# Layer 1's attention: the transposes of the probabilities and the values' product one row of scores later, the rotation of the queries behind the second row

## The chip, the cores and the metric

One core of a Trainium2 chip runs the whole program: four small transformer layers with different attention and feed-forward parts, as a single launch. The metric is the device time of that launch in microseconds. Its engines work in parallel, each through its own instruction stream in order: TensorE (PE, matmuls and transposes; its weight loads are shown apart as PEld), VectorE (DVE), ScalarE (ACT), GpSimd (POOL) and SyncE (SP), the last two here mostly issuing transfers. An instruction waits on semaphores for what it needs from other engines, and everything behind it on its engine waits with it.

## The reference

The input is x of 4 sequences, 512 tokens, 256 channels, in float32. Each of the four layers computes `x = x + attention(layernorm(x)) + ffn(layernorm(x))`. The change is in layer 1's attention, a latent attention with 16 heads:

```python
q = _rmsnorm(x @ wq_a, q_a_ln_w) @ wq_b            # 192 latent -> 16 heads x (128 + 64)
q_nope, q_pe = (q[..., :D_NOPE], q[..., D_NOPE:])
ckv = x @ wkv_a
compressed_kv, k_pe = (ckv[..., :KV_LORA], ckv[..., KV_LORA:])   # 64 + 64
kv = _rmsnorm(compressed_kv, kv_a_ln_w) @ wkv_b
k_nope, v = (kv[..., :D_NOPE], kv[..., D_NOPE:])
q_pe, k_pe = rope(q_pe), rope(k_pe)                 # rotation: x * cos + half_swapped(x) * sin
scores = jnp.einsum('bqhd,bkhd->bhqk', qf, kf) * softmax_scale   # causal
attn = jax.nn.softmax(scores, axis=-1)
out = jnp.einsum('bhqk,bkhd->bqhd', attn, v)
return out.reshape(b, s, N_HEADS * D_V) @ wo
```

Layer 1's feed-forward part is a mixture of 512 tiny experts chosen by product keys (8 per token, whose rows are gathered from memory), plus a dense gated unit. Layer 2's routing starts while layer 1 still runs.

## The kernel before, in words

The residual x and its normalised transpose xnT stay on chip. Layer 1 is written as four Python generators, which `weave` (L566) interleaves: each `yield` names a cost, and the stream with the smallest share of its declared total goes next. They are latent attention (`latent_pieces`, L1071, total 457), product keys and experts (`product_key_pieces`, 237), the dense unit (`glu_units`, 126) and layer 2's first routing (`room`, 270, from 0.915 of its total on). The order in which the generators write instructions is the priority that a list scheduler works with: it puts each engine's stream into its final order by readiness in a model of its own, so an instruction may stand earlier or later on its engine than it was written. Instructions marked with `keep_in_program_order` keep their order among each other.

Latent attention is computed with the key up-projection folded into the queries, and the value up-projection into the output weights. A *head* s here is one of 16 heads of one of 4 sequences: 64 of them, in 32 pairs; even and odd s make a pair. kf holds keys (64 latent channels and 64 rotated ones) of all tokens, cv the 64 latent value channels.

- `queries(p)` makes the queries of pair p: two PE products of two matmuls each (L1129 to L1134), a copy of the rotary part on ACT (L1137, pes), four transfers on SP that swap its halves of 32 (psw<-pes, L1139), and two scaled copies on ACT into qf (L1141, L1142).
- `rotate` finishes them on DVE: pes times cosine (L1148), psw times sine (L1149), two sums into qf (L1150, L1151).
- `probabilities(s, i)` makes row block i (128 queries) of head s against its (i + 1) x 128 keys: the score matmul on PE (L1042), mask and minimum on DVE (L1045), exponential and sum on ACT (L1049). After row 2 the reciprocals of the first three sums are taken on DVE (L1165) and the three tiles scaled on ACT (L1167), after row 3 the fourth. A *row of scores* is one such row block; a head has four. The tiles are called pr0 to pr3, with two buffers each.
- `turned(s, j)` transposes, on PE (L1174), key block j of the probabilities, out of the tiles j to 3, into one PSUM bank of two (tag tr), and returns a copy into PT (L1178): on DVE for even j (512 and 256 wide), on ACT for odd j (384 and 128). The copy of one j is written behind the transposes of the next.
- The values' product (L1328) multiplies the PT tiles of both heads of a pair with cv, eight matmuls; both heads run side by side in the two halves of PE's columns. ACT scales the result into zT (L1334).
- `out_pieces` multiplies the zT of two pairs with the output weights (L1282) and adds to x on DVE (L212).

The main loop runs over s from 0 to 64 and, inside, over the rows i. A step (s, i) writes row i of head s's scores, then `turned(s - 1, i)`, then the copy that was left from the step before, and yields 0.85. At odd s and i = 0 the rotation of the next pair's queries comes before that yield; at even s and i = 0 `queries` follows it, with a yield of 2.6. Every second step also lets a piece of `out_pieces` run. After the four steps of an even s (from 2 on) comes the values' product of heads s - 2 and s - 1, with a yield of 2.1:

```python
if s > 0:
    ...
    ready, copy = copy, turned(s - 1, i)
    if ready:
        ready()
if i == 0 and s % 2 == 1 and s < 63:
    rotate(*turning)
yield 0.85
```

Line numbers are those of the kernel before, unless said otherwise.

Of the kernel before, what the change touches and what calls it, by code (L numbers as in the profile page):

```python
# [16 lines left out]
P = 128  # L17
NB, SEQ, DM = 4, 512, 256
NT = NB * SEQ
NTILE = NT // P  # L20
TPB = SEQ // P
# [1049 lines left out]
def latent_pieces(c, a, keep, open_pool):  # L1071
# [20 lines left out]
    pool = open_pool()  # L1092
    weights = {}

    def carry(g):

        w = c.unit(a["l_units"][g])
        wqT, wkT, wvT = v3(w[:, :768], QL), v3(w[:, 768:1024], KL), v3(w[:, 1024:1280], KL)
        wo = v3(w[:, 1792:2816], DM)
        pw, pv = c.ps(), c.ps()  # L1100
        for h in range(4):
            hk = slice(h * KL, (h + 1) * KL)
            nc.tensor.matmul(pw[:, hk], lhsT=wqT[:, h, :P], rhs=wkT[:, h, :], start=True, stop=True)
            nc.tensor.matmul(
                pv[(h % 2) * KL : (h % 2 + 1) * KL, (h // 2) * DM : (h // 2 + 1) * DM],
                lhsT=wvT[:, h, :], rhs=wo[:, h, :], start=True, stop=True,
            )
        pw1 = c.ps()
        for h in range(4):
            hk = slice(h * KL, (h + 1) * KL)  # L1110
            nc.tensor.matmul(pw1[KL:, hk], lhsT=wqT[:, h, P:], rhs=wkT[:, h, :], start=True, stop=True)
        wl0 = c.tile(pool, [P, 256], "wl0")
        wl1 = c.tile(pool, [P, 256], "wl1")
        wz = c.tile(pool, [P, 2, DM], "wz")
        nc.scalar.copy(wl0, pw[:, :256])
        nc.scalar.copy(wl1[KL:, :], pw1[KL:, :256])
        nc.scalar.copy(wz, v3(pv, DM))
        weights[g] = w[:, 1280:1536], w[:KL, 1536:1792], wl0, wl1, wz

    def queries(p):  # L1120

        g, b, pair = p // 8, p // 2 % 4, p % 2
        if p % 8 == 0:
            carry(g)
        wpe0, wpe1, wl0, wl1, _ = weights[g]
        tokens = slice(b * SEQ, (b + 1) * SEQ)
        cols = slice(pair * P, (pair + 1) * P)
        pe, pl = c.ps(), c.ps()
        nc.tensor.matmul(pl, lhsT=wl0[:, cols], rhs=qa0[:, tokens], start=True, stop=False)  # L1129
        upper = nc.tensor.matmul(pe, lhsT=wpe1[:, cols], rhs=qa1[:KL, tokens], start=True, stop=False)  # L1130
        with tc.issue_after(upper.ins), tc.high_priority(offset=200):
            nc.tensor.matmul(pl, lhsT=wl1[KL:, cols], rhs=qa1[KL:, tokens], start=False, stop=True)
        with tc.high_priority(offset=100):
            nc.tensor.matmul(pe, lhsT=wpe0[:, cols], rhs=qa0[:, tokens], start=False, stop=True)  # L1134

        pes, psw = (c.tile(pool, [P, SEQ], n, bufs=1) for n in ("pes", "psw"))
        nc.scalar.copy(pes, pe)  # L1137
        for to in range(0, P, 32):
            nc.sync.dma_start(psw[to : to + 32, :], pes[to ^ 32 : (to ^ 32) + 32, :])  # L1139
        qf = c.tile(pool, [P, 2, SEQ], "qf")  # L1140
        nc.scalar.mul(qf[:KL, 0, :], pl[:KL, :], -scale)  # L1141
        nc.scalar.mul(qf[KL:, 1, :], pl[KL:, :], -scale)  # L1142
        qfs[p] = qf
        return pes, psw, qf

    def rotate(pes, psw, qf):
        pec = c.tile(pool, [P, SEQ], "pec", bufs=1)
        nc.vector.tensor_mul(pec, pes, cosq)  # L1148
        tc.keep_in_program_order(nc.vector.tensor_mul(psw, psw, sinq))  # L1149
        nc.vector.tensor_add(qf[:KL, 1, :], pec[:KL, :], psw[:KL, :])  # L1150
        nc.vector.tensor_add(qf[KL:, 0, :], pec[KL:, :], psw[KL:, :])  # L1151

    def probabilities(s, i):
        p, h = s // 2, s % 2
        b = p // 2 % 4
        if i == 0:
            totals[s] = c.tile(pool, [P, TPB], "total")
        rinv = totals[s]
        prs[s].append(exp_scores(
            c, pool, late, qfs[p][:, h, :], kf[:, h, b * SEQ : (b + 1) * SEQ], i, rinv[:, i : i + 1]  # L1160
        ))
        if i >= TPB - 2:

            done = slice(0, i + 1) if i < TPB - 1 else slice(i, i + 1)
            nc.vector.reciprocal(rinv[:, done], rinv[:, done])  # L1165
            for j in range(TPB)[done]:
                nc.scalar.mul(prs[s][j], prs[s][j], rinv[:, j : j + 1])  # L1167

    def turned(s, j):

        pt = c.ps("tr")
        n = SEQ - j * P
        for i in range(j, TPB):
            nc.tensor.transpose(  # L1174
                pt[:, (i - j) * P : (i - j + 1) * P], prs[s][i][:, j * P : (j + 1) * P], c.ident
            )
        copy = nc.scalar.copy if j % 2 else nc.vector.tensor_copy
        return lambda: copy(PTs[s][:, START[j] : START[j] + n], pt[:, :n])  # L1178

    START = (0, 512, 896, 1152)  # L1180
    qfs, prs, totals, PTs, zTs = {}, {}, {}, {}, {}
# [84 lines left out]
    turning = queries(0)  # L1266
# [23 lines left out]

    copy, pieces = None, iter(())
    yield 1.9
    for s in range(65):
        if s < 64:
            prs[s] = []
        for i in range(TPB):
            if s < 64:
                probabilities(s, i)
            if s > 0:
                if i == 0:  # L1300
                    PTs[s - 1] = c.tile(pool, [P, 1280], "PT")
                ready, copy = copy, turned(s - 1, i)
                if ready:
                    ready()
            if i == 0 and s % 2 == 1 and s < 63:
                rotate(*turning)
            yield 0.85
            if i % 2:
                yield from islice(pieces, 1)
            if i == 0 and s % 2 == 0 and s < 62:  # L1310
                turning = queries(s // 2 + 1)
                yield 2.6
        if copy:
            copy()
            copy = None
        if s > 0:
            del prs[s - 1]
        if s % 2 == 1:
            continue
        if s == 0:  # L1320
            continue

        p = s // 2 - 1
        g, b, pair = p // 8, p // 2 % 4, p % 2
        z = c.ps("acc")
        for j in range(TPB):
            for h in range(2):
                tc.keep_in_program_order(nc.tensor.matmul(  # L1328
                    z[h * KL : (h + 1) * KL, j * P :], lhsT=cv[:, b * TPB + j, :],
                    rhs=PTs[s - 2 + h][:, START[j] : START[j] + SEQ - j * P],  # L1330
                    start=(j == 0), stop=(j == TPB - 1),
                ))
        zTs[pair] = c.tile(pool, [P, SEQ], "zT", bufs=3)
        nc.scalar.mul(zTs[pair], z, kv_w)  # L1334
        yield 2.1
        if pair == 1:
            pieces = out_pieces(g, b)
# [1176 lines left out]
```

## Time and profile before

| | |
|---|---|
| median of 3 runs | 2913.95 us (2909.5 to 2915.22) |
| profiled execution | 2915.69 us |
| its span, first to last instruction | 2913.9 us |
| mean granted TensorE clock | 0.996 |
| busy share of the span: PE, DVE, ACT, POOL | 98%, 73%, 48%, 30% |
| layer 1's attention stage, 845 to 1450 us: PE, DVE, ACT busy | 588.7, 494.6, 411.8 of 605 us |

The profile is one execution, recorded instruction by instruction. Its page gives busy times, the chain of work that ended last and the costliest groups; the trace behind it also answers with tables by stretch of time, with lists of who waited for whom, and with the instructions in order of time. In the list of waits a line reads "engine, tile and line that waited, the engine, tile and line that released it: total us, number of times, longest". In the order of time a line has the start and length in us, engine, line, operation, out<-in, shapes and count, and in brackets the idle time before it with what ended it. PE's matmuls are pipelined and the ends shown are modelled, so a PE that shows as busy is not always at its peak.

### The profile page before, as it was taken

The page shows a single profiled execution, that of the slowest core. Times are in us where ns is not written, and L with a number is a line of the kernel's source. Part 1 is how long each engine was busy: PE and PEld are TensorE (multiplying, and loading weights), DVE is VectorE, ACT ScalarE, POOL GpSimd, SP SyncE. Part 2 cuts the span into 40 slices and gives each one's busy share as a digit, 9 for nine tenths or more (in the row PEclk, how much of TensorE's full clock was granted, in tenths as well). Part 3 has the DMA queues.
Part 4 walks back from the last instruction along what each step waited for, and adds up shares of the span by engine and source line. Part 5 has one row for each costly group of instructions (what it writes and reads, how often), then busy time and mean ns, then how long its engine had stood idle before and what let it go on. Part 6 is the DMA issues. An engine that isn't in the chain of part 4 may idle for free.

```text
span 2913.9 us, 40511 instructions
## 1 busy us (share of the span) xinstructions
PE 2860.2 (98%) x13767; PEld 1920.8 (66%) x13767; DVE 2131.7 (73%) x5421; ACT 1401.9 (48%) x3354; POOL 862.4 (30%) x687
## 2 busy tenths in 40 slices
PE   9999999999999999999999999999999999999999
PEld 5566665666655655555577688888888756666666
DVE  6778778787778787888775687777777666666666
ACT  4444445454366666667733554444444333333332
POOL 0565655656510033333035100000000043333331
PEclk9999999999999999999999999999999999999999
DMA  2433333333320144444234544444444300000000
GB/s 106 119 109 115 113 98 95 109 116 97 109 82 17 54 101 124 116 107 112 79 120 120 164 118 125 144 130 130 147 124 141 102 1 22 22 22 22 22 1 30
DMA packets 138687, 268.60 MB, mean 92 GB/s; under 512 B 19729, under 2 KB 99105, under 8 KB 134129
## 3 DMA queue, kind: packets, MB, share of 16 engines
q1 hardware_dynamic: 124016, 218.20, 24.4%
q0 software_dynamic: 14176, 47.04, 6.5%
q8 instruction: 109, 1.79, 0.3%
q14 instruction: 98, 0.79, 0.1%
q10 hardware_dynamic: 288, 0.79, 0.1%
HBM read 202.25 MB, written 54.26 MB: 88 GB/s over the span
## 4 chain that ended last, share of the span: by engine, by line
PE 59%; DVE 7%; ACT 4%; DMA 2%; issue 1%; SPq 0%; POOL 0%; DVEq 0%; ACTq 0%
PE mm L358 17%; PE acc L358 7%; PE mm L1042 6%; PE tr L358 6%; PE acc L1709 5%; PE acc L1058 4%; PE mm L177 3%; PE acc L266 1%; PE acc L1328 1%; DVE pr L1045 1%; PE tr L1174 1%; ACT pr L1049 1%; PE mm L185 1%; PE mm L2121 1%; ACT pr L1167 1%
## 5 line engine op out<-in xcount | busy, mean ns | idle before, releaser
L1049 ACT ACTIVATE pr<-pr,nm 128x128 f32<-128x128 f32 (+3 forms) x512 | 286.4, 560 | 297.6 <-DVE nm L1045 293.4
L1045 DVE CUSTOM_DVE_ANT_0 pr<-mm,late 128x128 f32<-128x128 f32 (+3 forms) x512 | 246.0, 483 | 115.9 <-PE mm L1042 114.3
L177 PE MATMUL mm<-xnT,wu 128*128 128x512 f32 x624 | 283.2, 595 | 0.9 <-DVE cy L620 0.5
L369 ACT COPY part<-mm 128x512 f32<-128x512 f32 (+1 forms) x372 | 177.9, 479 | 210.8 <-PE mm L358 202.6
L358 PE MATMUL mm<-token_sums,unit_sums 128*128 128x512 f32 (+1 forms) x624 | 268.1, 512 | 3.6 <-ACT part L369 3.6
L1435 POOL DMA_INDIRECT e<-in_p_experts,ids x128 | 127.7, 998 | 463.7 <-DVE x L206 358.3
L177 PE MATMUL mm<-xnT,w_in 128*128 128x512 f32 x512 | 230.9, 594 | 2.8 <-DVE cy L620 2.8
L520 DVE SCALAR_TENSOR_TENSOR x<-acc,cw,x 128x128 f32<-128x128 f32 x372 | 128.7, 346 | 106.8 <-PE acc L358 105.1
L177 PEld LDWEIGHTS mm<-xnT,wu 128*128 128x128 f32 x624 | 115.4, 190 | 126.6 <-issue 117.9
L620 DVE SCALAR_TENSOR_TENSOR cy<-mm,ws,cy 128x509 f32<-128x509 f32 (+2 forms) x216 | 159.8, 744 | 40.9 <-ACT cy L616 37.1
L1042 PE MATMUL mm<-kf,qf 128*128 128x128 f32 (+3 forms) x512 | 180.2, 443 | 3.8 <-DVE nm L1045 1.9
L785 ACT ACTIVATE xD<-xc,ws 128x128 f32<-128x128 f32 x256 | 83.6, 390 | 193.3 <-POOL y L826 182.8
L802 POOL TENSOR_TENSOR G<-G,CB 128x1024 f32<-128x1024 f32 x64 | 151.1, 2361 | 76.8 <-DVE G L765 76.8
L1042 PE MATMUL mm<-k,q 128*128 128x128 f32 (+3 forms) x512 | 170.5, 438 | 2.6 <-DVE nm L1045 2.3
L358 PEld LDWEIGHTS acc<-down_sums,hidden_sums 128*128 128x128 f32 x744 | 111.7, 191 | 85.1 <-issue 83.4
L177 PEld LDWEIGHTS mm<-xnT,w_in 128*128 128x128 f32 x512 | 95.8, 190 | 107.2 <-issue 91.8
L1709 PEld LDWEIGHTS acc<-PT,V 128*128 128x128 f32 x1280 | 153.8, 193 | 5.1 <-issue 1.7
L1709 PE MATMUL acc<-PT,V 128*128 128x128 f32 x1280 | 153.9, 276 | 0.0
L302 POOL TENSOR_TENSOR down_sums<-wu 128x256 f32<-128x256 f32 x8 | 5.8, 730 | 498.4 <-DMA wu<-in_o_units 498.4
L765 DVE TENSOR_TENSOR_SCAN G<-G,eye 128x1024 f32<-128x1024 f32 x64 | 147.2, 2300 | 0.1
L1174 PEld LDWEIGHTS tr<-con,pr 128*128 128x128 f32 x640 | 82.3, 141 | 89.9 <-ACT pr L1167 26.7
L503 DVE TENSOR_TENSOR whole<-mm,part 128x512 f32<-128x512 f32 x128 | 88.5, 692 | 68.9 <-PE mm L358 68.9
(456 smaller groups left out, 6735.1 us busy)
## 6 DMA issues: line engine op xcount, KB each, us to landing
turned<-Y SPq DMA_DIRECT2D x252, 160.0 KB, 2.6
PT<-turned SPq DMA_DIRECT2D x63, 640.0 KB, 3.9
G<-own SPq DMA_DIRECT2D x64, 512.0 KB, 4.7
w_in<-in_m_units SPq DMA_DIRECT2D x16, 1024.0 KB, 5.9
eb<-since SPq DMA_DIRECT2D x96, 128.0 KB, 3.5
wu<-in_o_units SPq DMA_DIRECT2D x6, 1536.0 KB, 6.6
wo<-in_m_units SPq DMA_DIRECT2D x16, 512.0 KB, 4.3
psw<-pes SPq DMA_DIRECT2D x128, 64.0 KB, 2.0
```

Of the source, the lines that this page charges most:

```text
L177: c.nc.tensor.matmul(out, lhsT=w[:, d, cols], rhs=c.xnT[:, d, tokens], start=(d == 0), stop=(d == 1))
L358: self.kept(self.c.nc.tensor.matmul(bank, lhsT=lhsT, rhs=rhs, start=first, stop=True, skip_group_check=not first))
L369: self.c.nc.scalar.copy(r, bank)
L520: c.nc.vector.scalar_tensor_tensor(x, bank, self.factor(u, tt), x, ALU.mult, ALU.add)
L620: nc.vector.scalar_tensor_tensor(y[:, j:], src[:, : SEQ - j], conv[:, k, 3 - j : 4 - j], y[:, j:], ALU.mult, ALU.add,)
L765: tc.keep_in_program_order(nc.vector.tensor_tensor_scan(flat, flat, eye.rearrange("p h t -> p (h t)"), 0.0, ALU.mult, ALU.add))
L802: nc.gpsimd.tensor_mul(G, G, seqs[b][2][:, t, :][:, None, :].to_broadcast([P, HG, P]))
L1042: kept(nc.tensor.matmul(sc, lhsT=q[:, i * P : n], rhs=k[:, :n], start=True, stop=True))
L1045: nc.vector.tensor_tensor_reduce(out=pr, in0=sc, in1=late[:, SEQ - n :], scale=scale, scalar=-NEG, op0=ALU.add, op1=ALU.min, accum_out=nm,)
L1049: nc.scalar.activation(pr, pr, AF.Exp, bias=nm, scale=-1.0, accum_out=total)
L1435: nc.gpsimd.indirect_dma_start(out=e, out_offset=None, in_=a["p_experts"], in_offset=bass.IndirectOffsetOnAxis(ap=ids[:, t, k : k + 1], ax ...
L1709: kept(nc.tensor.matmul(zs[:, i], lhsT=head["V"][:, j, h, :], rhs=head["PT"][:, :, i * (i + 1) // 2 + j, :], start=(j == 0), stop=(j == i),))
```

## The change

The double loop over s and i becomes one loop over 261 steps n, with s and i from n. A step writes its row of scores as before; but the transposes it writes are those of step n - 5 instead of step n - 4: `turned(s, 0)` now comes behind the second row of head s + 1, and `turned(s, 3)` behind the first row of head s + 2. The copies move with them. The values' product follows the last copy of an odd head as before, so it is written behind the first row of an odd head instead of behind the last row of an even one. The rotation is written at i = 1 of odd heads instead of i = 0. The score rows, the queries, the dense unit and the experts keep their places among the steps; the pieces of the output projection still run at i = 1 and 3.

```diff
-    for s in range(65):
+    for n in range(4 * 65 + 1):
+        s, i = divmod(n, TPB)
         if s < 64:
-            prs[s] = []
-        for i in range(TPB):
-            if s < 64:
-                probabilities(s, i)
-            if s > 0:
-                if i == 0:
-                    PTs[s - 1] = c.tile(pool, [P, 1280], "PT")
-                ready, copy = copy, turned(s - 1, i)
-                if ready:
-                    ready()
-            if i == 0 and s % 2 == 1 and s < 63:
-                rotate(*turning)
-            yield 0.85
-            if i % 2:
-                yield from islice(pieces, 1)
-            if i == 0 and s % 2 == 0 and s < 62:
-                turning = queries(s // 2 + 1)
-                yield 2.6
-        if copy:
-            copy()
-            copy = None
-        if s > 0:
-            del prs[s - 1]
-        if s % 2 == 1:
+            if i == 0:
+                prs[s] = []
+            probabilities(s, i)
+        done, j = divmod(n - TPB - 1, TPB)
+        if done >= 0:
+            if j == 0:
+                PTs[done] = c.tile(pool, [P, 1280], "PT")
+            ready, copy = copy, turned(done, j)
+            if ready:
+                ready()
+        if i == 1 and s % 2 == 1 and s < 63:
+            rotate(*turning)
+        yield 0.85
+        if i % 2:
+            yield from islice(pieces, 1)
+        if i == 0 and s % 2 == 0 and s < 62:
+            turning = queries(s // 2 + 1)
+            yield 2.6
+        if done < 0 or j < TPB - 1:
             continue
-        if s == 0:
+        copy()
+        copy = None
+        del prs[done]
+        if done % 2 == 0:
             continue
 
-        p = s // 2 - 1
+        p = done // 2
         g, b, pair = p // 8, p // 2 % 4, p % 2
         z = c.ps("acc")
 ...
-                    rhs=PTs[s - 2 + h][:, START[j] : START[j] + SEQ - j * P],
+                    rhs=PTs[done - 1 + h][:, START[j] : START[j] + SEQ - j * P],
```

## The prediction

> **What bounds the kernel now.** First the page: TensorE (PE) is busy nearly throughout, so a gain has to come out of PE's own time.
>
> ```profile
> span 2913.9 us, 40511 instructions
> PE 2860.2 (98%) x13767; PEld 1920.8 (66%) x13767; DVE 2131.7 (73%) x5421; ACT 1401.9 (48%) x3354; POOL 862.4 (30%) x687
> ```
>
> Then the table by stage, for the stage that the change touches, layer 1's attention (its score matmuls, L1042, run from 845 to 1446 us). Columns: length; busy time of PE, PEld, DVE, ACT, POOL (instructions in brackets); granted clock, DMA share, GB/s.
>
> ```profile
> 845.00:1450.00 605.00, 588.69 (x2678) 342.51 (x2680) 494.57 (x1721) 411.81 (x1091) 120.81 (x122) 0.99 0.34 90
> ```
>
> PE has 16.3 us without work here; DVE has 110, ACT 193. PE's waits, and those of its weight loads (PEld), in the same window:
>
> ```profile
> PE tr L1174 <- ACT pr L1167: 4.9, 12, 1.5
> PE tr L1174 <- ACT PT L1178: 3.5, 4, 1.4
> PE tr L1174 <- DVE PT L1178: 0.9, 4, 0.3
> ```
>
> ```profile
> PEld tr L1174 <- ACT pr L1167: 25.9, 65, 2.0
> ```
>
> PE counts as idle only when its pipeline has drained, so 4.9 us understates the first line. Taking starts of matmuls against the spacing at which they follow each other undisturbed (each is two instructions; 0.22 us for 128 columns, 0.43, 0.65, 0.86 for 256, 384, 512), I find 34 late starts of transposes behind scaled probabilities, 13.2 us together. That is the stock the change can draw on. One of them in the order of time (head 37, PE, ACT and DVE):
>
> ```profile
> 1204.97 1.02 PE L1042 MATMUL mm<-kf,qf 128*128 128x512 f32 x2
> ...
> 1206.26 0.68 DVE L1045 CUSTOM_DVE_ANT_0 pr<-mm,late 128x512 f32<-128x512 f32 x1
> ...
> 1206.99 0.72 ACT L1049 ACTIVATE pr<-pr,nm 128x512 f32<-128x512 f32 x1
> ...
> 1207.67 0.38 PE L1042 MATMUL mm<-kf,qf 128*128 128x128 f32 x2
> 1207.71 1.90 ACT L1167 ACTIVATE pr<-pr,total 128x128 f32<-128x128 f32 x4
> ...
> 1208.14 0.14 PEld L1174 LDWEIGHTS tr<-con,pr 128*128 128x128 f32 x1 [0.28 <-ACT pr L1167]
> 1208.15 0.33 PE L1174 MATMUL tr<-con,pr 128*128 128x128 f32 x1
> ```
>
> Last score, minimum on DVE, exponential on ACT, then the four scalings; PE reaches the first transpose before the first scaling is out.
>
> **The chain that must fit.** A head's last score ends; 0.20 later DVE starts its 0.68; ACT takes 0.72 and 0.19 for the sum; the four scalings take 1.9. With DVE and ACT free (a third of the heads) the first scaled tile is there 2.04 us after the score's end and the last 3.56. Over the 64 heads the medians are 2.2 and 4.0, because DVE or ACT comes late.
>
> **The time PE fills meanwhile**, from the order of PE's instructions in both builds and the spacings above, from the end of head s's last score to the first transpose of s, and to the first that reads its last tile. Even heads, typical, before: transpose 0.22, values' product 2.15, score 0.22 = 2.6; after: two transposes 0.43, score 0.22, transpose 0.22, product 2.15, score 0.43 = 3.4. Medians over all heads:
> - even: first 2.6 to 3.4, last tile 4.5 to 4.5 (before, more work stands between the transposes);
> - odd: first 3.0 to 5.6, last tile 4.7 to 6.2 (the queries' matmuls now come ahead).
>
> **The change, part by part.**
>
> 1. *Transposes later.* No instruction is added or removed; 640 transposes and 256 copies move. Subtracting, head by head, that head's own two chain times from PE's filling gives 12.9 us of waits before (15.7 with 0.1 us for the signal; the trace has 13.2). With the changed fillings it gives 8.9 (10.7). In that I charge a new wait: in 27 of the 32 even heads the copy of the previous head's last transpose now stands on ACT ahead of this head's last exponential and must wait for a transpose that comes behind the next score, so the exponential starts at 1.28 us instead of 0.92, and the last tile is out at 3.92 at the earliest. Queued behind it are four scalings and then PE. Even heads go from 3.8 to 5.2, odd ones from 9.2 to 3.7. I take -4.5; bounds -13.2 (all gone) and +9 (the slower rival below).
>
> 2. *The clock.* The longest of these waits has a sequel:
>
> ```profile
> 1130.68 0.87 PE L1174 MATMUL tr<-con,pr 128*128 128x128 f32 x2 [1.50 <-ACT pr L1167]
> ```
>
> and the stretch right after it, in the table by stretches (columns as above):
>
> ```profile
> 1130.80:1137.60 6.80, 6.80 (x25) 4.06 (x26) 3.48 (x13) 2.24 (x7) 4.22 (x5) 0.50 0.65 172
> ```
>
> For 6.8 us the granted clock was 0.50, so 3.4 us were lost. It began with DVE held 3.44 us by an expert's row, which made ACT late. The head concerned has PE filling of 2.7 and 4.5 before, 5.2 and 5.8 after, against a chain of 4.8 and 6.3: its wait falls from 2.1 to 0.5. I take -3.4; bounds -5.1 (the 3.4 us at half clock from 1444.8 go too) and +3.4 (a new episode). [...] The row shows 1.5 us of idleness just before the fall.
>
> 3. *Transpose banks.* A transpose also waits until the copy of the one two before it has freed its bank: 3.5 + 0.9 us above. Lower quartile of the filling for the wide copy on DVE (0.69 us): 1.72 to 2.15; for the 384-wide one on ACT (0.47): 1.93 to 1.50 in odd heads. I take -1; bounds -4.4, +4.4.
>
> 4. *Values' product.* It still follows the last transpose of its pair; its last two matmuls start 1.6 us in, and the 128-wide copy takes 0.25, so no new wait. But the output projection (L1282) now follows one row sooner, and ACT's scaling of the product (L1334, 0.67) stands behind one more exponential (0.39 + 0.19). The scaled product was ready some 1.6 us after the product; make that 2.2. Filling at the 16 places: median 2.6 before; now 2.4 at most, but 1.5 to 1.9 at five, each losing 0.3 to 0.7. I take +2.5; bounds 0 and 16 x 0.58 = +9.
>
> 5. *Rotation behind the second row.* Four DVE instructions move. DVE waits 16.8 us in this stage for the half-swapped queries (13 waits). But the scheduler places that product by when it believes the transfer landed: DVE work between the independent product (L1148) and the dependent one (L1149) averages 3.6 us before, 3.7 after. So 0; bounds -3 and +3 (two PE stalls of 1.6 and 1.3 us hang on those waits). The queries' four transfers and ACT copies stay behind the first row of even heads; POOL's order is unchanged, SP's differs in a few neighbouring issues at the start; cover: PE has other work there, else their 2.0 us landing shows.
>
> 6. *One step more at the end* (261 for 260). After head 63's last score the same 20 transposes, two products and the projection remain: 0; bounds -1, +1.
>
> Sum: -4.5 - 3.4 - 1 + 2.5 = -6.4. The profiled execution took 2915.7 us (2913.9 span, 1.8 around it), so 2909.3 by it; it lies 1.7 above the median of the runs, so 2907.5 against 2913.95.
>
> **The rivals.**
> - *Little moves.* The scheduler had interleaved transposes and scores already, even heads gain nothing, the half-clock episode survives: -4.5 - 1 + 2.5 = -3: 2911. For: last-tile medians of even heads are equal. Against: odd heads hold 9.2 of 12.9 us and gain 1.5 us each.
> - *Slower: ACT's queue.* The copy ahead of the last exponential delays it in every even head rather than only where ACT was early. At 0.36 us each, waits are 13.8 us, no gain; at 0.8 us, 22 to 25, that is +9, with +2.5 and -1 from parts 4 and 3: 2924. It decides from about 0.6 us. For: 27 heads, and DVE's reciprocal behind the exponential waits too (L1165, 8.4 us now). Against: the transpose it waits for ends only 0.9 us after the score.
> - *All waits go:* -13.2 - 3.4 - 2 = -18.6: 2895. Against: even heads keep 4.5 us of filling while 17 of their 32 chains exceed 4.1.
>
> **How the numbers follow.** What can be told from no change is about 0.2%, 5.8 us. Forecast (2902 to 2911 by itself) 0.45; little moves 0.23; slower 0.21; all waits go 0.11. A third of the forecast's and most of the second's chance lies within 5.8 us; the rest of the forecast and the last case are faster: faster 0.46, same 0.33, slower 0.21. Bounds of parts 3 to 6 add some 5 us either way to the forecast; leaving out a tenth on each side gives 2896 to 2922.
>
> **What would show it.** Right: transposes' waits for scaled probabilities fall from 25.9 us (PEld) to under 18; no half clock near 1130; stage 845 to 1450 shorter by 5 to 8 us, other stages equal. The zT step: a new wait of L1282 for ACT's L1334 scaling. Part 5: DVE's wait for the swapped queries stays at 13 to 20 us. Wrong: ACT waiting for transposes (its PT copies) above today's 21 us with exponentials behind, more half-clock stretches, or a stage no shorter though the waits fell, which would mean that matmul waits had only hidden each other.

## The result, and the profile after

The kernel before took 2913.6 us, the changed one 2919.6 us (medians of 12 runs each): ratio 1.0022, 95% interval 1.0015 to 1.0029. That is 6 us more, where 6.4 less was forecast; it lies inside the range and on the wrong side. Run twice more, on two different chips, the change came out at 1.0016 (1.0005 to 1.0026) and 1.0022 (1.0011 to 1.0033). So it is slower, by 3 to 8 us, just about at the bound below which nothing can be told.

The lines of the page of the kernel after, span and busy times:

```profile
span 2917.0 us, 40524 instructions
PE 2857.9 (98%) x13767; PEld 1925.9 (66%) x13767; DVE 2133.4 (73%) x5421; ACT 1404.3 (48%) x3354; POOL 863.0 (30%) x687
```

Busy times are those of before within 0.3%: no work was added, something waits differently. The table by stretches (length; busy time of PE, PEld, DVE, ACT, POOL; granted clock, DMA share, GB/s), for the stage and for the stretch that had half clock before:

```profile
845.00:1450.00 605.00, 582.13 (x2666) 345.05 (x2664) 493.13 (x1719) 411.16 (x1081) 121.28 (x122) 0.99 0.35 90
1130.80:1137.60 6.80, 6.80 (x42) 4.75 (x40) 4.74 (x16) 4.88 (x15) 5.11 (x6) 1.00 0.65 150
```

The half clock at 1130.8 is gone, as forecast. The list of waits of the kernel after (engine, tile and line that waits, what released it: total us, times, longest) shows the first step done too, and two new waits. First PEld and PE, 845 to 1450 us:

```profile
PEld tr L1174 <- ACT pr L1167: 10.0, 19, 1.8
```

```profile
PE tr L1174 <- DVE PT L1178: 3.5, 7, 1.4
PE tr L1174 <- ACT pr L1167: 3.4, 7, 1.1
PE tr L159 <- ACT xnT L164: 3.0, 1, 3.0
PE acc L1327 <- DVE PT L1178: 2.9, 3, 1.1
PE tr L1174 <- ACT PT L1178: 2.7, 3, 1.4
```

The weight loads of the transposes wait 10.0 us for scaled probabilities instead of 25.9. Two lines stand there that the prediction doesn't have: the values' product (L1327, the old L1328) waits for a copy by DVE, and the transposes of a layer norm (L159) wait for ACT. Both waits were small in the kernel before:

```profile
PE tr L159 <- ACT PT L1178: 1.2, 1, 1.2
PE acc L1328 <- DVE PT L1178: 0.2, 1, 0.2
```

L159 belongs to layer 2: `layernorm` runs for each sequence as soon as layer 1 is done with it, late in this stage, and its transposes take turns in the same two PSUM banks (tag tr) as those of the probabilities.

**An account of PE's late starts.** As in the prediction, I take the start of each matmul against the spacing at which they follow each other undisturbed, and sum what is above it, by the matmul that is late, from 845 to 1475 us. Time lost to half clock is in these sums where it falls on such a matmul. In us:

| | transposes | scores | values' product | output projection | layer norm | sum | time against before |
|---|---|---|---|---|---|---|---|
| before | 26.1 | 13.6 | 6.3 | 0.9 | 2.7 | 49.6 | |
| change, first | 20.2 | 10.7 | 11.4 | 1.2 | 10.0 | 53.5 | +6.0 |
| change, e5 | 20.9 | 10.2 | 11.7 | 1.2 | 9.8 | 53.8 | +3.3 |
| change, e13 | 20.3 | 10.5 | 12.1 | 1.2 | 9.7 | 53.8 | +7.8 |
| e6, old lag from head 56 | 21.5 | 11.2 | 11.9 | 1.2 | 4.2 | 50.0 | +1.0 |
| e17, that and a later product | 27.1 | 6.0 | 8.6 | 2.5 | 2.3 | 46.5 | -1.5 |
| e8, before without the swap | 19.3 | 9.7 | 7.2 | 0.9 | 2.9 | 40.0 | -13.5 |
| e7, change without the swap | 16.8 | 9.5 | 7.2 | 1.1 | 8.2 | 42.8 | -10.0 |

The last column is the difference of the medians. The transposes gained 5 to 6 us and the scores 3; the product gave 5 to 6 back, the layer norm 7. Each of these entries repeats within 1 us in three profiles of the change, so they belong to its order of instructions and not to one execution. That their net of +4 is about the size of the loss is no proof. PE's other matmuls, which the table leaves out, are late by some 3 us less in the change than in the profile of before, mostly in stretches at half clock; and that profile lost 10.9 us to half clock, where the mean of later runs of the same kernel is 8.1 and 8.3 (e5 and e13, below). So the profiled executions hardly differ: spans of 2917.0, 2913.2 and 2913.7 us for the change, 2913.9 for before. The table says where waits came and went; what a place costs has to come from the experiments.

**The two places.** The product's wait, PE and DVE in the order of time in the kernel after (start, length, engine, line, operation, and in brackets the idle time before it with what ended it):

```profile
1252.43 0.38 PE L1174 MATMUL tr<-con,pr 128*128 128x128 f32 x2
...
1252.65 0.39 PE L1042 MATMUL mm<-kf,qf 128*128 128x128 f32 x2
...
1252.88 0.27 PE L1174 MATMUL tr<-con,pr 128*128 128x128 f32 x1
...
1253.08 2.15 PE L1327 MATMUL acc<-PT,cv 128*64 128x512 f32 x10
...
1254.38 0.69 DVE L1149 TENSOR_TENSOR psw<-psw,tab 128x512 f32<-128x512 f32 x1 [2.35 <-DMA psw<-pes]
...
1254.99 0.68 DVE L1045 CUSTOM_DVE_ANT_0 pr<-mm,late 128x512 f32<-128x512 f32 x1
...
1255.88 0.42 DVE L1178 COPY PT<-tr 128x256 f32<-128x256 f32 x1
...
1256.35 0.86 PE L1327 MATMUL acc<-PT,cv 128*64 128x256 f32 x6 [1.12 <-DVE PT L1178]
```

DVE stands 2.35 us at the sine product for the swapped queries; behind it in its queue are a 512-wide minimum, a reciprocal, another minimum and then the copy for which the product's last three matmuls (six instructions) wait. Before, a 512-wide score (0.86 us) stood between the transposes that this copy reads and the product; now it is the 128-wide first score of the next head (0.22), so by these spacings the copy has 0.64 us less. The same place in the kernel before, PE:

```profile
1251.75 0.38 PE L1174 MATMUL tr<-con,pr 128*128 128x128 f32 x2
1251.97 1.02 PE L1042 MATMUL mm<-kf,qf 128*128 128x512 f32 x2
1252.83 0.27 PE L1174 MATMUL tr<-con,pr 128*128 128x128 f32 x1
1253.03 2.38 PE L1328 MATMUL acc<-PT,cv 128*64 128x512 f32 x16
```

All sixteen instructions of the product run there without a break. The layer norm's wait, in the kernel after:

```profile
1405.06 0.33 PE L1174 MATMUL tr<-con,pr 128*128 128x128 f32 x1 [0.27 <-DVE PT L1178]
...
1406.30 0.63 PE L159 MATMUL tr<-con,xn 128*128 128x128 f32 x4 [0.17 <-DVE PT L1178]
...
1406.44 0.71 ACT L1049 ACTIVATE pr<-pr,nm 128x512 f32<-128x512 f32 x1
...
1407.14 1.90 ACT L1167 ACTIVATE pr<-pr,total 128x128 f32<-128x128 f32 x4
...
1409.34 0.56 ACT L164 COPY xnT<-tr 128x512 f32<-128x512 f32 x1
1409.80 0.26 ACT L1178 COPY PT<-tr 128x128 f32<-128x128 f32 x1
1409.95 0.60 PEld L159 LDWEIGHTS tr<-con,xn 128*128 128x128 f32 x4 [3.26 <-ACT xnT L164]
```

Both banks are full at 1406.9: one with the last transpose of a head, one with the first half of the layer norm. ACT empties them only behind an exponential, four scalings and another exponential. PE stands 3.0 us, and half clock follows at once (1410.1). At a second place PE's transposes of the layer norm stand 3.1 us until DVE's copy (L1178) frees a bank, and half clock follows again (1451.1):

```profile
1410.10:1413.50 3.40, 3.40 (x26) 1.86 (x27) 2.07 (x3) 0.85 (x2) 0.00 (x0) 0.50 0.04 10
1451.10:1454.50 3.40, 2.95 (x7) 1.48 (x7) 2.90 (x12) 2.71 (x7) 0.00 (x0) 0.50 0.00 0
```

**A third place, at the start of the stage.** Twenty us into the stage two waits of transposes fall close together in the kernel after, and half clock follows. PE in the order of time:

```profile
865.59 0.52 PE L1174 MATMUL tr<-con,pr 128*128 128x128 f32 x3 [0.66 <-DVE PT L1178]
867.19 0.33 PE L1174 MATMUL tr<-con,pr 128*128 128x128 f32 x1 [1.08 <-ACT pr L1167]
```

The table by stretches, columns as above:

```profile
867.40:870.80 3.40, 3.40 (x9) 1.85 (x10) 2.38 (x16) 0.52 (x2) 0.00 (x0) 0.50 0.06 7
```

The other two profiles of the change have it too (half clock from 863.8 and 864.4), the profile of before does not. It stands in none of the theories below, and no experiment was made for it.

### The profile page after: what moved, and what is told of

Same layout as the page of the kernel before. It is cut to its first block, busy times and chain, and to the rows that moved or that the text cites. A ratio compares the mean times of both kernels' runs of the same rounds, so it can differ in the third digit from the quotient of the medians.

```text
span 2917.0 us, 40524 instructions
## 1 busy us (share of the span) xinstructions
PE 2857.9 (98%) x13767; PEld 1925.9 (66%) x13767; DVE 2133.4 (73%) x5421; ACT 1404.3 (48%) x3354; POOL 863.0 (30%) x687
## 4 chain that ended last, share of the span: by engine, by line
PE 61%; DVE 5%; ACT 3%; DMA 2%; issue 1%; SPq 0%; DVEq 0%; ACTq 0%; POOL 0%; POOLq 0%
PE mm L358 17%; PE mm L1042 7%; PE acc L358 7%; PE tr L358 6%; PE acc L1708 5%; PE acc L1058 4%; PE mm L177 3%; PE acc L266 2%; PE acc L1327 2%; PE tr L1174 1%; PE acc L1282 1%; PE mm L2120 1%; PE mm L185 1%; DMA psw<-pes 1%; ACT pr L1167 1%
## 5 line engine op out<-in xcount | busy, mean ns | idle before, releaser
L1174 PEld LDWEIGHTS tr<-con,pr 128*128 128x128 f32 x640 | 82.4, 142 | 76.8 <-issue 24.6
```

## The experiments

The theories: **R**, the rotation behind the second row puts DVE's wait for the swap in front of the copies; **N**, the lag meets the layer norm's transposes at the end; **A**, the slower rival of the prediction, ACT's queue; **V**, nothing but where half clocks happen to fall; later **P**, the product's wait for DVE's copy is the other half of the loss; **D**, writing the product later only hands that wait on; **S**, DVE's standing still for the swap makes the others late; and **Q**, the rotation alone has a small gain. The chips differ: on those of e5 to e8, e13 to e16 and e17 to e18 the kernel before took 2911.9, 2910.8 and 2910.1 us, about as at first; on those of e1 to e4 and e9 to e12 it took 2943.6 and 2947.7. Ratios are against before on the same chip. Where two experiments are compared directly, the difference is that of their means, with a 95% interval from drawing the runs of both again and again.

### e1, e2: one part of the change alone

```diff
-        if i == 1 and s % 2 == 1 and s < 63:    # e1, on the change
+        if i == 0 and s % 2 == 1 and s < 63:
-            if i == 0 and s % 2 == 1 and s < 63:    # e2, on the kernel before
+            if i == 1 and s % 2 == 1 and s < 63:
```

> The change without its second part: the transposes, the copies and the values' product come one row later, the rotation of the queries stays behind the first row of odd heads. Before is 2913.6, the change 2919.6. Theory R (the rotation behind the second row brings DVE's wait for the swapped queries ahead of the copies that the values' product needs; 3.8 us of new waits of that product for DVE's copy in the profile): no slower than before, 2909 to 2914, and those waits of the values' product under 1 us. Theory N (the lag leaves transposes of probabilities in the two banks when layer 2's layer norm wants them; 8.5 us of waits of the layer norm's transposes and 3.4 us of half clock twice at 1410 and 1451): as slow as the change, 2917 to 2921, with these waits still there. Theory A (the last exponential waits on ACT behind a copy): 2917 to 2921 too, with waits of transposes for scaled probabilities above those of the change (3.4 us in PE's list).

> The kernel before with the rotation of the queries behind the second row of odd heads, nothing else. Theory R: slower than before by 3 to 6 us, 2916.5 to 2919.5, with waits of the values' product for DVE's copy of PT. Theories N and A: within 2 us of before, 2911.5 to 2915.5.

Measured: e1 1.0001 (0.9990 to 1.0011), e2 0.9986 (0.9974 to 0.9998). The rotation alone costs nothing; if anything it gains (4.1 us by the medians). e1 took no longer than before, as R had it and N had not; but of R the rest fails: e2 lost nothing, and with the rotation at its old place the late starts of the product are 16.5 us in e1, more than the 11.4 to 12.1 of the change elsewhere. A falls: PE's weight loads wait less for scaled probabilities with the lag than without it (10.0 against 25.9 us in the first pair of profiles, 9.3 against 25.7 in e1 and e2, 845 to 1490 us). But these runs fell on a chip 30 us slower, where the waits are others: with the lag the transposes' late starts are 28.6 us (e1), without it 32.1 and 39.2 (e2, e4). What the whole change does there was not run, so e1 doesn't say whether lag and rotation add up. Lag and rotation were parted on slower chips alone (e1, e2, e12).

### e3, e4: the layer norm's transposes in other banks

```diff
-        c.parts(3, lambda b: layernorm(c, b, halves[...]))
+        c.parts(3, lambda b: layernorm(c, b, halves[...], apart=True))
```

> The change, with the transposes of layer 2's layer norm in the PSUM banks of the scores instead of the two that the probabilities' transposes use (and the second of each pair two steps later). Theory N: the 8.5 us of waits of those transposes go to under 2 us and the half clocks at 1410 and 1451 with them (1.7 us each): 6 to 10 us faster than the change, 2910 to 2914. Theories R and A: within 2 us of the change, 2917.5 to 2921.5, the waits moved to other instructions.

> The control to the last one: the kernel before with the same edit to the layer norm. All theories: within 2 us of before, 2911.5 to 2915.5, since the waits of the layer norm's transposes were 2.5 us there; theory N gives a gain of at most 2.5 us and the half clock at 1444 (1.7 us) on top.

Measured: e3 (on the change) 0.9982 (0.9971 to 0.9992), e4 (on before) 1.0003 (0.9993 to 1.0014). It looked like N, with a gain of 5 us that the control doesn't have. On a chip like the first the same kernel (e14) has no gain; what e3 gained here stays open.

### e5, e6: the change again, and the old lag from head 56 on

```diff
-        done, j = divmod(n - TPB - 1, TPB)
+        m = n - TPB - (n <= 4 * 56)      # at n = 224 both m and m + 1
+        done, j = divmod(m, TPB)
```

> The change itself once more, to stand beside e1 to e4 where the kernel before took 2943.6 us (30 us more than at first, with the same instructions): there the lag alone was +0.0%, the rotation alone -0.14%, the change with the layer norm's transposes apart -0.18%, the control +0.03%. Theory N (clash with the layer norm's transposes): the change is slower than before by 4 to 7 us here too, and so 9 to 12 us above e3. Theory R (rotation): ruled out as the cause of a loss by e2, unless rotation and lag together lose what neither loses alone; then also +4 to +7. Theory V (the loss isn't a property of the change; the half-clock stretches and the experts' rows fall differently with any small shift in time): within 4 us of e3, that is faster than before by 0 to 9 us.

> The change, but from step 224 (head 56) on the transposes come at their old distance of four rows again; the rotation stays behind the second row. Theory N: the layer norm's transposes meet the order that they met before, so this keeps the gain of heads 20 to 55 (5 us in the first pair of profiles) and loses the price of the end: 4 to 7 us faster than the change, faster than before by up to 5 us. Theory V: within 3 us of the change.

Measured: e5 1.0016 (1.0005 to 1.0026), e6 1.0009 (0.9998 to 1.0020); e6 is 2.5 us faster than e5 (0.8 to 4.2). V falls, since the loss came again with the same waits at the same places. Waits of PE from 845 to 1470 us in e5:

```profile
PE tr L159 <- ACT xnT L164: 3.7, 2, 3.0
...
PE tr L159 <- DVE PT L1178: 3.3, 2, 3.1
```

and in e6:

```profile
PE acc L1333 <- DVE PT L1178: 3.8, 3, 2.3
...
PE tr L159 <- ACT PT L1178: 1.2, 1, 1.2
PE tr L159 <- ACT xnT L164: 0.8, 1, 0.8
```

The 2.5 us are under N's 4 to 7 and within what V allowed, so the size alone decides nothing; the waits above do: those of the layer norm's transposes fall from 7 to 2 us. So the lag at the end of the stage costs 2.5 us here, about half of the loss; the waits of the product (L1333 in this file) stay.

### e7, e8: without the swap of the rotary halves

The four transfers are left out and the sine product reads the copy itself, so the rotation is not the reference's.

```diff
-        for to in range(0, P, 32):
-            nc.sync.dma_start(psw[to : to + 32, :], pes[to ^ 32 : (to ^ 32) + 32, :])
-        tc.keep_in_program_order(nc.vector.tensor_mul(psw, psw, sinq))
+        tc.keep_in_program_order(nc.vector.tensor_mul(psw, pes, sinq))
```

> The change without the four transfers that swap the halves of the rotary queries: the sine product reads the copy itself, so DVE never waits for a transfer there (the output is wrong for it). In the first profile of the change DVE waited 20.3 us for these transfers in the stage, and 3.8 us of the values' product's waits stood behind them. Theory R: 4 us or more faster than the change, and more than the same edit gains on the kernel before. Theories N and V: 0 to 3 us faster, as much as on the kernel before; DVE has slack.

> The same edit on the kernel before (16.8 us of DVE's waits, output wrong). Theory R: 0 to 2 us faster than before. Theories N and V: 0 to 3 us faster, the same as the edit gains on the change.

Measured: e7 (change) 0.9967 (0.9956 to 0.9977), e8 (before) 0.9958 (0.9943 to 0.9973). No theory had a gain of this size: 13 us on both. Without DVE's waits the change is still slower than before by 3.4 us (2.2 to 4.6); with them it is 3.3 by the medians: R falls a second time. But it tells what those waits do. Without them the product has no wait for DVE's copy left in the change, and its late starts are 7.2 us in both kernels; in the kernel before the same edit took 6.8 us from the transposes and 3.9 from the scores. In the change (e7 against e5) it took 4.1 us from the transposes and 4.5 from the product. DVE stands still for the swap in both; before, transposes and scores are late for it, in the change transposes and the product. What remains between e7 and e8 is the layer norm, 8.2 against 2.9, and half clock. PE in e7:

```profile
PE tr L159 <- DVE PT L1176: 3.1, 1, 3.1
PE tr L1172 <- ACT PT L1176: 3.0, 6, 1.0
PE tr L159 <- ACT PT L1176: 2.8, 1, 2.8
```

### e9 to e12: the product later, both mended, the end alone, the rotation again

```diff
             probabilities(s, i)
+        if due is not None:              # e9, on the change; e10, on e6
+            new, due = product(due), None
+            yield 2.1
+            pieces = new or pieces
...
-        done, j = divmod(n - TPB - 1, TPB)    # e11: lag 4 up to step 224, 5 behind it
+        done, j = divmod(n - TPB - (n > 4 * 56), TPB)
```

> The change, with the values' product written one score row later still, behind the second row of odd heads (so that a 256-wide score, 0.43 us, more stands between the last transposes and the product). In both profiles of the change the product waits 7 to 8 us inside for DVE's 256-wide copy (2.7 before), and e6, which kept the old end, kept those waits (and took 1.0 us more than before). Theory P (this wait is the other half of the loss): the product's inner waits fall to under 4 us, 3 to 5 us faster than the change, so within 2 us of before. Theory D (PE's order only passes the wait on to the transposes behind it): within 2 us of the change, 2 to 6 us slower than before, with the transposes' late starts 3 to 5 us up.

> Product one row later and the old distance from head 56 on, together. Theories N and P: both losses go, so the gain on the transposes' waits is left: 1 to 5 us faster than before. Theories N and D: as e6, 0 to 3 us slower than before.

> The kernel before up to head 55, the change's order from head 56 on (the complement of e6, whose end was the old one). Theory N: the whole price of the end and none of the gain: 2 to 6 us slower than before, with the waits of the layer norm's transposes of 6 to 9 us and half clock behind them. Theory V: within 2 us of before.

> The rotation alone, as in e2, where it was 4 us faster on a chip on which the kernel before took 30 us more. Theory R would have it 3 to 6 us slower than before; theory Q (its own, small gain: DVE does rows of scores first while the transfers land) 2 to 5 us faster; theories N, P and V within 2 us of before.

Measured, again on a slower chip (2947.7 us): e9 0.9993 (0.9984 to 1.0002), e10 0.9980 (0.9969 to 0.9990), e11 1.0018 (1.0009 to 1.0027), e12 0.9998 (0.9988 to 1.0008). e11 has only the end of the change (from head 56 on its rotation is behind the second row too, and at step 224 nothing is transposed), and is 5.2 us slower than before: the price of the end is confirmed from the other side, and e9 less e10 gives it a third time, 4.6 us (2.0 to 7.1). For the product the times speak for P: e9 lies 2.0 us under before by the medians and e10 6.7, where P had within 2 us of before for e9 and 1 to 5 us faster for e10, and D had both slower than before. The waits speak for D in part: in e9 and e10 the output projection (L1282), which needs the scaled product, took over 12 us of late starts, where the change has 1 on the first kind of chip. Some of this is the chip's, since e12, with the product at its old place, waits there as well. PE in e10, then in e12:

```profile
PE acc L1282 <- ACT zT L1303: 7.4, 3, 4.1
```

```profile
PE acc L1282 <- ACT zT L1334: 3.3, 3, 1.7
```

e12 didn't repeat the gain of e2: the rotation alone is between nothing and -0.14%.

### e13 to e16: change and mended change on one chip, the sine product on POOL

e13 is the change, e14 is e3 again, e15 and e16 have, on the kernel before and on e14:

```diff
-        tc.keep_in_program_order(nc.vector.tensor_mul(psw, psw, sinq))
+        nc.gpsimd.tensor_mul(psw, psw, sinq)
```

> The change once more, beside the next three. Where the kernel before takes some 2912 us: 2915 to 2920, slower by 3 to 6 us, with waits of the layer norm's transposes of 8 to 10 us and inner waits of the values' product of 7 to 8 us. Where the kernel before takes 2944 us or more (experts' rows late, waits of transposes for scaled probabilities 30 us instead of 24): the lag is worth more there; by e3 less what e11 gives for the end, -5.2 + 5.2, within 3 us of before.

> As e3, to stand beside the change on the same chip. Theory N: 2 to 6 us faster than e13; then the rest of the loss is what the product's wait for DVE takes from the transposes' gain, and it is within 3 us of before where that takes 2912, and 3 to 7 us faster where it takes 2944. Theory V: within 2 us of e13.

> The kernel before with one edit: the product of the swapped queries with the sine runs on POOL, so that it is POOL and not DVE that waits for the swap (16.8 us of DVE's waits in the stage, and 32 x 0.69 us of DVE's work). Theory S (DVE's standing still for the swap is what makes transposes and scores late before, and the values' product in the change): 4 to 13 us faster than before (e8, without the swap, was 13.5 us faster), late starts of transposes and scores down by 4 us each. Against: POOL issues the experts' gathers in the same stream, and one waiting there holds the product up: then PE waits at the scores for the queries, and it is 0 to 10 us slower.

> The change with the layer norm's transposes apart and the sine product on POOL. Theory S: the product's inner waits fall to under 2 us (as without the swap, where they were gone), 4 to 13 us faster than e14, and about as fast as e15: the lag itself is then worth within 3 us either way. If the lag has a gain of its own that the two waits hid, 3 to 8 us faster than e15.

Measured: e13 1.0022 (1.0011 to 1.0033), e14 1.0032 (1.0021 to 1.0043). Own banks for the layer norm are no remedy: its late starts fall from 9.7 to 4.3 us, those of the transposes rise from 20.3 to 24.6 and those of the product from 12.1 to 13.9. PE in e14:

```profile
PE tr L1174 <- DVE PT L1178: 4.9, 8, 1.4
PE tr L1174 <- ACT PT L1178: 4.7, 4, 2.2
...
PE mm L159 <- DVE xn L149: 3.5, 2, 2.2
```

So on this chip the part of N that blamed the banks is wrong: with banks of their own the matmuls wait for the same two engines, ACT and DVE. What N keeps is that the lag at the end costs (e6, e11, e9 against e10). Which piece of that order does it was not separated further.

e15 took 1.0104 (1.0089 to 1.0120), e16 1.0132 (1.0116 to 1.0147): S wasn't tested, because the edit did what its own doubt said, and more: 29 and 38 us of loss, where the doubt had 0 to 10. POOL and DVE in e15:

```profile
POOL psw L1149 <- DMA psw<-pes: 226.7, 19, 24.3
POOL e L1435 <- DVE x L206: 122.4, 39, 17.4
```

```profile
DVE qf L1150 <- POOL psw L1149: 44.4, 19, 4.7
```

POOL issues the experts' gathers in the same stream; the two kinds of waiting hold each other up, and DVE waits 44.4 us for POOL where it waited 16.8 for the transfer.

### e17, e18: both mended on a chip like the first, and the output projection later too

e17 is e10; e18 lets the pieces of the output projection run at `i % 2 == 0`.

> As e10 (product one row later, old distance from head 56 on), which was 0.2% faster than a before of 2948 us; wanted where the kernel before takes some 2912 us. Theories N and P: the product's inner waits fall from 8 us to under 4, the layer norm's from 10 to under 5, and it is 2 to 5 us faster than before. Theory D: the stalls stand elsewhere (the output projection for the scaled product, 12 us of late starts in e10; transposes), and it is within 2 us of e6, that is 0 to 3 us slower than before.

> The same, with the pieces of the output projection at the even rows (i = 0 and 2) instead of the odd ones, so that two more transposes and a score stand between the values' product and the projection that needs it. If the projection's wait for the scaled product (12 us of late starts in e10, 1 us in the change) is what the later product paid with: 4 to 8 us faster than e17, with those late starts under 4 us. Theory D: within 2 us of e17, the late starts moved on to the transposes.

Measured: e17 0.9991 (0.9982 to 1.0001), e18 1.0002 (0.9993 to 1.0012). Against their own befores e6 lies at +0.09% and e17 at -0.09%, so the later product is worth some 2.5 to 5 us on top of the old end (by the medians or by the ratios), if the two chips may be compared. With both places mended the loss is gone. P had said 2 to 5 us faster than before, and it is 1.5 by the medians; D had said 0 to 3 slower. The row of e17 in the account shows how: product -3.3 and scores -5.2 against e6, but transposes +5.6, so part of the wait was handed on, as D has it. The projection's 12 us of e10 are 2.5 here. e18 took them to 1.5 and was 2.2 us slower than e17 (0.3 to 4.0), near D's bound of 2; its new waits are at the scores rather than at the transposes. PE in e18:

```profile
PE mm L1042 <- DVE sg L220: 1.7, 1, 1.7
```

Of the orders that were run, that of e17 is the best: 0.1% under before here, 0.2% on the slower chip (e10), and the first is within what can't be told from no change.

## Why the prediction was wrong

1. *Transposes later* (part 1, -4.5), with *transpose banks* (part 3, -1): **right**. Late starts of all transposes fell by 5.2 to 5.9 us in three profiles, where -5.5 was the sum; the weight loads' wait for scaled probabilities went from 25.9 to 10.0 us. Some of the fall, about 1 to 2 us, lies in stretches at half clock and belongs to part 2, so these two parts were rather 4 than 5.5. The new wait of ACT that was charged there came: its copies (PT, L1178) wait 38.2 us for transposes instead of 21.4. ACT in the kernel after and before, 845 to 1450:

```profile
ACT PT L1178 <- PE tr L1174: 38.2, 42, 3.8
```

```profile
ACT PT L1178 <- PE tr L1174: 21.4, 19, 3.6
```

The prediction named this, above 21 us, as a mark of the slower rival (ACT's queue). It wasn't one: PE's waits for scaled probabilities fell all the same. A wait of an engine with slack is no mark by itself. That the scores would gain 3 us was not foreseen.

2. *The clock* (part 2, -3.4): the stretch at 1130.8 is in none of the three profiles of the change, but the term had the wrong sign. From span times (1 - granted clock), averaged over the runs, half clock cost 9.7 and 12.0 us in the change (e5, e13) against 8.1 and 8.3 in the kernel before beside it: +1.6 and +3.7. The step that failed was to take the half clocks of one execution (10.9 us in the profile of before) as a standing cost of the kernel, and to count only those that the change would remove. All three profiles of the change have half clock beginning at 864 to 867, 1407 to 1410 and 1642 to 1646 us, some 1.7 us of loss each, where that of before has none. The upper bound, +3.4 for a new episode, was nearer.

3. *Values' product* (part 4, +2.5, "so no new wait"): **the step that failed**. It looked only at the last copy, 128 wide on ACT, and at the scaled product behind. The copy in front of it, 256 wide on DVE, lost 0.64 us of cover and stands behind DVE's wait for the swap: product +5.1 to +5.8 us. The wait that was charged, the projection for the scaled product, rose by 0.3 us of late starts in the change; it came (12 us) when the product was moved further on a slower chip, in e9 and e10. What the product's wait costs in time is known only from e17 against e6, on two chips, and is in that far argued.

4. *Rotation* (part 5, 0): right in itself (e2, e12: between -0.14% and nothing, both on slower chips); DVE's wait for the swap is 20.3 and 19.0 us (first profile and e5), at the edge of the 13 to 20 named. But "0" was right only for the waits on DVE: what stands behind them on DVE changed from minima to the product's copy, and the prediction didn't ask that.

5. *The end* (part 6, 0, bounds -1 and +1): **failed**, by more than its bounds. The working counted the attention's own last instructions and not what else runs there: layer 2's layer norm, in the same banks and behind the same ACT. Late starts +7, with two half clocks (the profile of before has two there as well, at 1444.8 and 1468.7); in time 2.5 us by e6, 3.4 in e7 against e8, 5.2 by e11, 4.6 by e9 against e10. Half clock, priced as in 2, is 1.5 us of the first (9.7 in e5, 8.3 in e6), all of the second (5.0 in e8, 8.7 in e7) and of the third (18.1 before, 23.6 in e11), but only 0.3 of the last. Which waits of the new order at the end are to blame stays open.

6. *The rivals.* "Little moves" is wrong, much moved. "Slower: ACT's queue" ended on the right side of no change by luck, with the wrong mechanism. A rival in which the gain of the transposes comes back at the product and at the layer norm was missing; it would have been read from one list, DVE's and ACT's instructions in front of every copy that the moved transposes need.

So the mechanism of the gain was right and measured, -8 to -9 us at transposes and scores, and it was returned where the new order meets the same two late engines: +5 at the product, +7 at the layer norm, in late starts, and in new half clock. The end's share is shown by experiments, the product's mostly by the waits, and what the start of the stage adds was not tested.

## What to carry to other kernels

When a consumer is moved later to let it arrive behind its producer, the lateness isn't gone: list every copy that the moved step needs, see what stands in front of it on its own engine's queue, and look for another user of its buffers anywhere in the program, above all where the next layer starts. If moving a step again moves part of the stall with it (product, projection, transposes, here), the engine that is late is what to work on: taking the swap's wait from DVE was worth 13 us in either order, more than any order of PE's instructions gave. And a half-clock stretch in one profile may be a draw: price it by the mean over runs (10.9 us in one profile of before, 8.1 and 8.3 as means of later runs), and call it the kernel's own when further profiles have it at the same place.

## What the runs showed of the hardware

**Where half clock fell in the profiles of before and after.** By the clock records of these two traces, up to 2890 us, the granted clock was 0.50 from 786.0, 1130.8, 1444.8, 1468.7 and 2284.5 us on before, and from 788.9, 867.4, 1410.1, 1451.1 and 1645.6 us on after, each time for 3.413 us or twice that. Within each execution these starts lie whole multiples of 3.413 us apart (101, 92, 7 and 239; 23, 159, 12 and 57). The length of a wait doesn't tell alone: PE's waits of 1.50 us at 1129.2 (before) and of 1.92, 3.02 and 3.09 us at 1642.6, 1406.9 and 1447.1 (after) were followed by half clock, those of 2.27 us at 1638.8 (before) and of 2.24 us at 1470.9 (after) were not. Cutting both executions into stretches of 3.413 us from these starts and taking PE's idle time in each, by the profile's modelled ends: three stretches at full clock had more than 2 us, and all three were followed by half clock; of eight with 1.5 to 2, five were; of 1669 with less, two, at 782.6 and 785.5 us, with 1.0. So in these two profiles the idleness that falls into one such stretch says more than the length of a wait, though between 1.5 and 2 us it doesn't decide. The 2.27 us of before stand across two stretches that meet at 1639.36, with 0.58 and 1.68 us of idleness.

In e5 a 1.92 us wait of the same layer 2 score for its minimum ended at 1640.66, and half clock followed (columns as above):

```profile
1638.70:1642.10 3.40, 1.48 (x5) 0.87 (x5) 3.13 (x14) 2.44 (x8) 0.00 (x0) 1.00 0.34 99
1642.10:1645.50 3.40, 3.40 (x16) 3.04 (x15) 1.45 (x8) 2.64 (x6) 0.00 (x0) 0.50 0.98 317
```

In e6 the wait, again of 1.92 us, ended at 1638.51, and the granted clock was 1.00 from 1638.7 to 1645.5.

**Chips differ more than the change does.** The same kernel before took 2910 to 2914 us in four sets of runs and 2944 and 2948 in the other two, each set on a chip of its own. The mean durations of instructions on DVE and ACT, and of POOL's issues of the experts' gathers, are the same there (from 845 to 1480 us, in groups of 20 and more, within 1.5% in e4, the kernel before but for its layer norm's banks); the waits for gathered rows of layer 2 are longer. PE's longest wait between 1470 and 1700 us in e4, for the transposed gathered rows of layer 2's experts:

```profile
PE mm L2121 <- ACT xsT L2114: 7.9, 4, 3.5
```

In the kernel before on a chip of the first kind:

```profile
PE mm L2121 <- ACT xsT L2114: 1.0, 2, 0.7
```

In layer 1 too waits are longer: late starts of the transposes are 32 to 39 us there without the lag (e2, e4) and 27.6 to 28.6 with it (e1, e3). That late rows are the reason isn't shown: the traces of these runs have no landing times, and DVE's waits for the rows of layer 1's experts are 6.4 us in e2 and e4 (845 to 1480) against 8.8 before. What is slower there stays open, and so does what the whole change would be worth there: it was not run on such a chip.
